# A message-passing layer on one core: copies of gathered columns from step 5 on, relu on VectorE, other places for zeros, lists and the last updates

## The chip, the core and the metric

The kernel runs on one core of one Trainium2 chip. The metric is the time of one execution in device microseconds. Engines are called PE (TensorE matmul) and PEld (its weight loads), DVE (VectorE), ACT (ScalarE), POOL (GpSimd) and SP (SyncE). POOL issues the indirect DMAs (gathers), SP most other DMAs, ACT a few.

## The reference

A graph with 12500 nodes of 64 features and 200000 edges of 32 features, the edges sorted by destination. For each edge a hidden vector of 128 is made from source node, destination node and edge; the messages are summed by destination; each node is updated, and the sum of old and new features is normalized.

```python
msg_in = concatenate([nodes[row], nodes[col], edge_features], axis=-1)   # row = src, col = dst
messages = relu(msg_in @ mW1 + mb1) @ mW2 + mb2
aggregated = segment_sum(messages, col, num_segments=12500)
upd = relu(concatenate([nodes, aggregated]) @ uW1 + ub1) @ uW2 + ub2
out = layernorm(nodes + upd)
```

## The kernel before

Edges are cut into 1563 tiles of 128, six tiles to a step (261 steps, index s), two steps to a group g of twelve tiles, for which DVE makes the selection masks. Everything is fp32.

**Tables.** Since the first layer is linear, the node parts of it are made once for every node: table A (nodes @ mW1[:64], used by source) and table B (nodes @ mW1[64:128] + mb1, used by destination), both in DRAM. `chunk_a` makes table A in thirteen chunks of eight blocks ahead of the loop (PE products, one half evacuated on ACT, L580, the other on DVE, L578, the write issued by ACT, L582). Table B is made chunk by chunk between steps (`chunk_b`, add at L588 on DVE), from step 11 to about step 50.

**A step.** `edge_part(s+1)` (L365) fills one PSUM tile `pc` with the edge and destination parts of the first layer. `node_part(s)` adds the source part: six gathers from table A (L207, one indirect DMA of 128 rows for each tile) landed in `xg`; DVE adds `xg` to `pc` and writes `h` (L392, or L388 in a copied step), and ACT applies relu to `h` (L393; L389 and L390 in a copied step). `collect(s-1)` multiplies `h` with the mask into `sums` (L420) and counts the edges (L425). In even steps `select(g+1)` makes the next masks on DVE (L233, L235, L241). The first ten steps gather node features instead and use PE for the source part (L282, L283, L381, L383).

**Copied tiles.** POOL issues one gather after another. To relieve it, some steps gather only four of their six tiles. For the other two the transposed node features are put together column by column in SBUF, in a tile `xc` of 128 columns (upper half one tile, lower half the other): `xtop` holds all nodes' features in its upper half and zeros below, `xbot` zeros above and features below, so that one column of `xc` is the sum (ACT, `singly`, L336, an activation with a bias) or the bitwise or (DVE, `joined`, L343) of one column of each. The column numbers are values in registers, loaded from the list `col_a` (L313, a register load of up to 16 values for eight copies). PE then multiplies `xc` by the weights into `pc` (L368). A step with this is a "group" in the copy plan: before, 96 of them, the first at step 16, at gaps of 3 and 2, 64 columns on ACT and 64 on DVE. The features for the second halves of `xtop` and `xbot` are loaded by `others` and their zeros written by DVE memsets in `zeros` (L562, L563), in steps 3 to 10; `columns_list` makes `col_a` in step 9.

**Order.** The order on each engine is the order of the code; waits are derived from the tiles. `xg` has nine buffers (`ROWB`): gathers of step s wait until step s-9 has been added. `pc`, `pu`, `py` and `pb` share two PSUM buffers, `h` and `xc` have two each.

**Updates.** The nodes are finished in 33 windows of up to 448 nodes (`UPD` lists the steps at which windows begin; every 4 steps near the end). `close` copies the sums (ACT, L439, L440), `update` and `activated` make the hidden layer (PE L462, L463, ACT L468), `residual` the output (PE L476, L477), `evacuate` copies it (ACT L483), `statistics`, `deviation`, `norm` (DVE L491, L493, L504, L507, ACT L498) normalize and `store` writes it, spread over the following steps.

Of the kernel before, what the change touches and what calls it, by code (L numbers as in the profile page):

```python
# [72 lines left out]
FIRST, GAPS = 16, (3, 2)  # L73
COPIED = []
while FIRST + sum(GAPS) * (len(COPIED) // len(GAPS)) + sum(GAPS[:len(COPIED) % len(GAPS)]) < NSUB - 6:
    COPIED.append(FIRST + sum(GAPS) * (len(COPIED) // len(GAPS)) + sum(GAPS[:len(COPIED) % len(GAPS)]))
RNDS = -(-len(COPIED) // len(GAPS))
LAST = 4 * (N - 1)
ACTS, CHUNK = 64, 8


def updates():


    def node(s):
        return N * min(1.0, s * SUB * P / E) ** 2
    at = [0]
    for s in range(1, NSUB):
        if s > at[-1] and node(s + 1) - node(at[-1]) > UN - WIN:
            at.append(s)  # L90
    return at
# [4 lines left out]
UL = min(UB, -(-int(N * (1 - (UPD[-1] * SUB * P / E) ** 2) + WIN) // P)) * P  # L96
# [3 lines left out]
def gnn_kernel(ctx: ExitStack, tc: tile.TileContext, x1T, x, eT, e_rows, src, src_row, dst, dst_row, wlist, wrow, wnext, whalf,  # L100
# [40 lines left out]

    cols = const.tile([RNDS * len(GAPS), 2 * P], I32, name="cols")
    col_a = const.tile([RNDS * len(GAPS), P, 2], I32, name="col_a")
# [68 lines left out]
    with tc.tile_pool(name="sup", bufs=2) as sup, tc.tile_pool(name="work", bufs=2) as work, tc.manual_schedule():  # L212
# [13 lines left out]
        def select(g, at=None):  # L226
# [11 lines left out]
            if at is not None:  # L238
                joined(at, 1, 3)
# [46 lines left out]
        def columns_list():  # L286

            for r in range(len(GAPS)):
                v = src_row[:, ((FIRST + sum(GAPS[:r])) * SUB + SUB - 2) * P:]
                nc.sync.dma_start(cols[r * RNDS:(r + 1) * RNDS],  # L290
                                  bass.AP(v.tensor, v.offset, [[sum(GAPS) * SUB * P, RNDS], [1, 2 * P]]))
            cv = cols.rearrange("k (b e) -> k b e", b=2)
            for b, base in enumerate((XBASE, YBASE)):
                nc.vector.tensor_scalar(col_a[:, :, b], cv[:, b], 4.0, float(base), op0=ALU.mult, op1=ALU.add)
# [3 lines left out]
        def portion(s, total, unit):  # L298

            rate, found = sum(GAPS) / len(GAPS), []  # L300
            begin = min(c - 2 - (j + 1) * rate for j, c in enumerate(COPIED[:len(GAPS)]))
            for j, c in enumerate(COPIED):
                lo, hi = (min(-(-int(total * (s + d - begin - j * rate) / rate * 16 + 0.5) // (16 * unit)) * unit, total) for d in (0, 1))
                lo = max(lo, 0)
                if lo < hi:
                    if c not in xc:
                        xc[c] = work.tile([P, P], F32, name="xc")
                    found.append((xc[c], j % len(GAPS) * RNDS + j // len(GAPS), lo, hi))
            return found

        def addresses(k, a, m, engine):

            _, v = nc.values_load_multi_w_load_instructions(  # L313
                col_a.rearrange("k e b -> k (e b)")[k:k + 1, 2 * a:2 * m], engines=[engine], min_val=XBASE,
                max_val=YBASE + LAST, skip_runtime_bounds_check_because="sources are node numbers")
# [15 lines left out]
        def singly(s, part, of):  # L331

            todo = [(o, k, e) for o, k, lo, hi in portion(s, ACTS, 2) for e in range(lo, hi, 2)]
# [4 lines left out]
        def joined(s, part, of):  # L338

            todo = [(o, k, ACTS + e) for o, k, lo, hi in portion(s, P - ACTS, 2) for e in range(lo, hi, 2)]  # L340
            for o, k, a, m in share(todo, part, of):
                for e, top, bot in addresses(k, a, m, ET.DVE):
                    nc.vector.tensor_tensor(o[:, e:e + 1].bitcast(I32), top.bitcast(I32), bot.bitcast(I32),  # L343
                                            op=ALU.bitwise_or)
# [26 lines left out]
        def node_part(s):  # L371
# [12 lines left out]
            else:  # L384
                a = xg.pop(s)[0].rearrange("p (b k) f -> p b k f", b=2)
                if s in COPIED:
                    m = SUB // 2 - 1
                    nc.vector.tensor_tensor(h[:, :, :m], pc[:, :, :m], a[:, :, :m], op=ALU.add)  # L388
                    nc.scalar.activation(h[:, :, :m], h[:, :, :m], AF.Relu)  # L389
                    nc.scalar.activation(h[:, :, m:], pc[:, :, m:], AF.Relu)  # L390
                for b, m in parts(n) if s not in COPIED else []:
                    nc.vector.tensor_tensor(h[:, b, :m], pc[:, b, :m], a[:, b, :m], op=ALU.add)  # L392
                    nc.scalar.activation(h[:, b, :m], h[:, b, :m], AF.Relu)  # L393
# [9 lines left out]
        def collect(s):  # L403
# [15 lines left out]
            for i in range(n):  # L419
                nc.tensor.matmul(ps[:, bass.ds(ws[i], WIN)], h[:, i % 2, i // 2, :], S[g][:, k0 + i, :],  # L420
                                 start=False, stop=ends and i == n - 1)
            if s == 0 or period[s - 1] != u:
                nc.tensor.matmul(pn, zero_b[:, 0:1], zero_b, start=True, stop=False)
            for i in range(n):
                nc.tensor.matmul(pn[:, bass.ds(ws[i], WIN)], one, SB[g][:, k0 + i, :, 1], start=False,  # L425
                                 stop=ends and i == n - 1)

# [8 lines left out]
        def close(u):  # L436

            ps, pn = sums.pop(u)
            nc.scalar.copy(sums_s[u % 2], ps)  # L439
            nc.scalar.copy(xw[u % 2][0:1, :UW], pn)  # L440
# [7 lines left out]
        def blocks(u):  # L448
            return UB if u + 1 < K else UL // P
# [8 lines left out]
        def update(u):  # L458
# [3 lines left out]
            nc.tensor.matmul(pu, w2u, sums_s[u % 2][:, :n], start=True, stop=False)  # L462
            nc.tensor.matmul(pu, uz, xw[u % 2][:, :n], start=False, stop=True)  # L463
# [8 lines left out]
        def residual(u):  # L472

            py = psum.tile([P, UB, D], F32, name="py", tag="pc")
            for i in range(blocks(u)):
                nc.tensor.matmul(py[:, i], xw[u % 2][:, i * P:(i + 1) * P], ux, start=True, stop=False)  # L476
                nc.tensor.matmul(py[:, i], hT[:, i * P:(i + 1) * P], u2, start=False, stop=True)  # L477
# [166 lines left out]
        for k, c in enumerate(range(0, NB, NCH)):  # L644
            chunk_a(c)
            if k == 0:
# [103 lines left out]
        for s in range(last + 2):  # L750
# [6 lines left out]
            def earlier(n):  # L757

                return next((u for d, u in due.items() if u + 1 < K and s - d == n - (u + 2 == K and n > 2)), None)
            if tail:  # L760
                norm(K - 1)
            if s + 2 < NSUB:
                windows(s + 2)
            if s < NSUB:
                node_part(s)
                joined(s, 0, 3 if j == 0 and g + 1 < NSUP else 2)
# [3 lines left out]
            if 1 <= s <= NSUB:  # L770
                collect(s - 1)
            if s + 1 in due:
# [11 lines left out]
            if s in due:  # L784
# [15 lines left out]
            joined(s, 2 if j == 0 and g + 1 < NSUP else 1, 3 if j == 0 and g + 1 < NSUP else 2)  # L800
            singly(s, 0, 1)
            if s in due and due[s] + 1 < K:
# [175 lines left out]
```

## Time and profile before

| | us |
|---|---|
| median of three runs | 1740.07 (1739.24 to 1740.65) |
| the profiled execution, its own time | 1740.13 |
| its span, from the first to the last instruction | 1738.4 |
| busy: PE, PEld | 1451.4, 1261.2 |
| busy: DVE, ACT | 1076.5, 1442.8 |
| busy: POOL | 1299.3 |
| mean granted TensorE clock | 0.574 of full speed |

Busy time is the time in which an engine executes; the reading and loading of registers, branches and the issue of DMAs do not count. A line of a group says line, engine, operation, tiles (out<-in), shapes and count, then busy us and mean ns of one, and behind the second bar the idle time of the engine just before such instructions, with what ended it. "issue" there is idle time in which the engine waited for nothing that the profile shows. In a timeline a line says start, duration, engine, line, operation, and in brackets the idle time ahead.

### The profile page before, as it was taken

Reading aid. Unit: us, or ns where it says so; the run is one execution under the profiler, and the core shown is the slowest. Engines: PE = TensorE matmul, PEld = TensorE weight load, DVE = VectorE, ACT = ScalarE, POOL = GpSimd, SP = SyncE. Lnnn points to the kernel's source line nnn. Section 1 sums busy time; section 2 is a strip of 40 time slices with the busy share of each in tenths; the row PEclk is TensorE's granted clock in tenths of the full one; section 3 lists DMA queues with packets and bytes.
Section 4 is the critical chain, followed back from the end, with each engine's and each line's share of the span. In section 5 each row is a group of like instructions: output and inputs, shape, how many; then the busy total and the mean of one; then the engine's idle time right before and its main releaser. Section 6 shows DMA issues by size and latency. Waiting matters only on the chain. (4 is left out here: it accounts for less than half of the span.)

```text
span 1738.4 us, 46326 instructions
## 1 busy us (share of the span) xinstructions
PE 1451.4 (83%) x9598; PEld 1261.2 (73%) x9598; DVE 1076.5 (62%) x7325; ACT 1442.8 (83%) x6691; POOL 1299.3 (75%) x1380
## 2 busy tenths in 40 slices
PE   3697888888888887887988889898888888889997
PEld 2586777878777776766877777687777667777775
DVE  1566766767676656666666666666666666666642
ACT  0216998999999888988999999999999999899941
POOL 7777777777777777777777777777777777777774
PEclk8665555565555555555555555555556656565665
DMA  8773434433333333333333333333333334343342
GB/s 214 207 160 103 124 105 128 120 92 100 101 97 98 95 97 94 98 101 95 99 107 103 104 107 104 105 106 104 105 108 109 106 109 111 104 111 110 108 111 63
DMA packets 207110, 192.27 MB, mean 111 GB/s; under 512 B 57098, under 2 KB 172931, under 8 KB 206835
## 3 DMA queue, kind: packets, MB, share of 16 engines
q1 hardware_dynamic: 148418, 92.38, 19.5%
q0 software_dynamic: 43872, 87.97, 18.5%
q10 hardware_dynamic: 14546, 8.93, 1.8%
q8 instruction: 91, 1.49, 0.4%
q14 instruction: 183, 1.50, 0.3%
HBM read 171.46 MB, written 17.66 MB: 109 GB/s over the span
## 5 line engine op out<-in xcount | busy, mean ns | idle before, releaser
L207 POOL DMA_INDIRECT xg<-tab_a,src_s x1311 | 1240.8, 946 | 399.6 <-issue 361.4
L336 ACT ACTIVATE xc<-xtop,xbot 128x1 f32 x6144 | 1167.3, 280 | 41.0 <-issue 29.8
L343 DVE TENSOR_TENSOR xc<-xtop,xbot 128x1 int32 x6144 | 536.7, 154 | 410.0 <-issue 397.1
L420 PEld LDWEIGHTS sums<-sel,h 128*128 128x128 f32 x3126 | 620.3, 299 | 73.8 <-ACT h L393 27.6
L420 PE MATMUL sums<-sel,h 128*128 128x32 f32 x3126 | 643.7, 373 | 27.0 <-ACT h L393 20.2
L365 PE MATMUL pc<-rhs,l 64*128 64x128 f32 x3126 | 424.7, 418 | 183.3 <-DVE h L392 128.3
L365 PEld LDWEIGHTS pc<-rhs,l 64*128 64x128 f32 x3126 | 353.1, 297 | 248.2 <-DVE h L392 144.9
L393 ACT ACTIVATE h<-h 128x768 f32<-128x768 f32 x156 | 129.6, 831 | 128.5 <-DVE h L392 127.9
L392 DVE TENSOR_TENSOR h<-pc,xg 128x768 f32<-128x768 f32 x156 | 148.0, 949 | 128.7 <-DMA xg<-tab_a,src_s 77.9
L235 DVE TENSOR_TENSOR l<-l,cps 128x768 f32<-128x768 int32 (+1 forms) x134 | 127.8, 953 | 7.8 <-DMA l<-in_dst_row 2.5
L425 PE MATMUL cnt<-sel,one 128*1 128x32 bf16 x1563 | 84.5, 187 | 0.0
L388 DVE TENSOR_TENSOR h<-pc,xg 128x512 f32<-128x512 f32 x96 | 66.1, 689 | 22.2 <-DMA xg<-tab_a,src_s 8.7
L241 DVE TENSOR_TENSOR sel<-cps,drc 128x384 f32<-128x384 f32 x131 | 71.6, 547 | 12.0 <-PE cnt L425 11.8
L368 PE MATMUL pc<-w1a,xc 64*128 64x128 f32 x384 | 74.3, 395 | 0.0
L462 PE MATMUL pu<-sums_s,w2u 128*128 128x448 f32 (+1 forms) x66 | 61.2, 1031 | 15.5 <-DVE h L392 14.9
L207 POOL DMA_INDIRECT xg<-in_x,src_s x60 | 57.5, 958 | 19.1 <-issue 18.0
L425 PEld LDWEIGHTS <-one 128*1 128x1 bf16 x1563 | 53.9, 83 | 22.1 <-issue 8.7
L476 PE MATMUL py<-ux,xw 128*128 128x64 f32 x262 | 66.3, 344 | 1.8 <-DVE h L392 1.8
L389 ACT ACTIVATE h<-h 128x512 f32<-128x512 f32 x96 | 59.2, 617 | 9.3 <-DVE h L388 9.0
L368 PEld LDWEIGHTS pc<-w1a,xc 64*128 64x128 f32 x384 | 66.2, 308 | 0.0
L477 PE MATMUL py<-u,hTu 128*128 128x64 f32 x262 | 65.0, 340 | 0.3 <-ACT hTu L468 0.3
L476 PEld LDWEIGHTS py<-ux,xw 128*128 128x128 f32 x262 | 53.0, 250 | 7.7 <-issue 3.1
(104 smaller groups left out, 749.4 us busy)
## 6 DMA issues: line engine op xcount, KB each, us to landing
l<-in_dst_row SPq DMA_DIRECT2D x262, 96.0 KB
l<-in_eT SPq DMA_DIRECT2D x262, 96.0 KB
xg<-tab_a,src_s POOLq DMA_INDIRECT x1311
rhs<-tab_b SPq DMA_DIRECT2D x361, 32.0 KB
tab_b<-tb SPq DMA_DIRECT2D x13, 512.0 KB
rhs<-tab_b SPq DMA_DIRECT2D x387, 16.0 KB
tab_a<-tb ACTq DMA_DIRECT2D x12, 512.0 KB
out<-y SPq DMA_DIRECT2D x32, 128.0 KB
```

Of the source, the lines that this page charges most:

```text
L207: nc.gpsimd.indirect_dma_start(out=a[:, i, :] if s < XG else a[:, i // 2, i % 2, :], out_offset=None, in_=A[:, :] if s >= XG else x[:, :], ...
L235: nc.vector.tensor_tensor(l[r], l[r].bitcast(I32), node[r].unsqueeze(2).broadcast_to([r.stop - r.start, SUP // 2, P]), op=ALU.is_equal)
L241: nc.vector.tensor_tensor(s[:, :nt], slot.unsqueeze(1).broadcast_to([P, nt, WIN]), drc[:, g * SUP:g * SUP + nt].unsqueeze(2).broadcast_to( ...
L336: nc.scalar.activation(o[:, e:e + 1], top.bitcast(F32), AF.Identity, bias=bot.bitcast(F32))
L343: nc.vector.tensor_tensor(o[:, e:e + 1].bitcast(I32), top.bitcast(I32), bot.bitcast(I32), op=ALU.bitwise_or)
L365: nc.tensor.matmul(pc[:, b, k, :], L[g][q:q + 64, m, :], rhs[g % 2][q:q + 64, w, :], start=s >= XG or k == 0, stop=s >= XG and not copied)
L368: nc.tensor.matmul(pc[:, b, k, :], xc[s][q:q + 64], w1a[q:q + 64], start=False, stop=True)
L392: nc.vector.tensor_tensor(h[:, b, :m], pc[:, b, :m], a[:, b, :m], op=ALU.add)
L393: nc.scalar.activation(h[:, b, :m], h[:, b, :m], AF.Relu)
L420: nc.tensor.matmul(ps[:, bass.ds(ws[i], WIN)], h[:, i % 2, i // 2, :], S[g][:, k0 + i, :], start=False, stop=ends and i == n - 1)
L425: nc.tensor.matmul(pn[:, bass.ds(ws[i], WIN)], one, SB[g][:, k0 + i, :, 1], start=False, stop=ends and i == n - 1)
L476: nc.tensor.matmul(py[:, i], xw[u % 2][:, i * P:(i + 1) * P], ux, start=True, stop=False)
```

## The change

- The copy plan: 110 groups instead of 96. Copying begins in step 5 (`BEGIN`), at a rate of 0.47 groups a step that falls to 0.42 (`RATES`). The first group is step 10, the last 254, and a group's copies end three steps ahead of it. ACT makes 68 of the 128 columns, DVE 60. Even steps get more of DVE's copies than odd ones (`SWING`).
- In `node_part` DVE adds `xg` into `pc` itself (PSUM) and then makes the relu from `pc` into `h`. Register loads for copies are placed between add and relu and behind the relu (`fetch`), the copies of both after that (`join`); eight more copies stand in `select`, and what is left of the step's share at the step's end.
- `zeros` are written by ACT, 14 pairs of 896 columns, one after each chunk of table A and two after the last. `others` go to steps 0 to 2, `columns_list` to step 2, and the list covers all steps.
- `collect` counts first and sums afterwards; `close` copies the counts first; `update` starts with the product of `xw`; `residual` makes all products of `xw` first.
- The last updates: windows begin at steps 244, 248, 252, 256 and 259 where they began at 245, 249, 253 and 257 (34 windows, the last one 192 nodes wide instead of 384). The update of the last window but one is made in one piece in step 259, ahead of that step's add.

```diff
-FIRST, GAPS = 16, (3, 2)
+BEGIN, FINAL = 5, 255
+RATES = 0.47, 0.42
+SWING = 0.04
+def progress(s, early=0.0):
+    s = max(s + 1 - BEGIN, 0)
+    return s * (RATES[0] + (RATES[1] - RATES[0]) * s / (2 * NSUB)) + (early if s else 0.0)
 COPIED = []
+for s in range(NSUB):
+    while min(progress(s), progress(s, -SWING if s % 2 else SWING)) >= len(COPIED) + 1 and s + 3 < FINAL:
+        COPIED.append(s + 3)
-ACTS, CHUNK = 64, 8
+ACTS, CHUNK = 68, 8
...
 def select(g, at=None):
-                joined(at, 1, 3)
+                join(fetch(quota(at), CHUNK))
...
+        def fetch(todo, n):
+            ready = []
+            while todo and n:
+                o, c, a = todo[0]
+                m = min(len([t for t in todo if t[1] == c]), n // 2)
+                del todo[:m]
+                n -= 2 * m
+                ready += [(o, *x) for x in addresses(c, a, a + 2 * m, ET.DVE)]
+            return ready
+        def join(ready):
+            for o, e, top, bot in ready:
+                nc.vector.tensor_tensor(o[:, e:e + 1].bitcast(I32), top.bitcast(I32), bot.bitcast(I32),
+                                        op=ALU.bitwise_or)
...
 def node_part(s):
-                if s in COPIED:
-                    m = SUB // 2 - 1
-                    nc.vector.tensor_tensor(h[:, :, :m], pc[:, :, :m], a[:, :, :m], op=ALU.add)
-                    nc.scalar.activation(h[:, :, :m], h[:, :, :m], AF.Relu)
-                    nc.scalar.activation(h[:, :, m:], pc[:, :, m:], AF.Relu)
-                for b, m in parts(n) if s not in COPIED else []:
-                    nc.vector.tensor_tensor(h[:, b, :m], pc[:, b, :m], a[:, b, :m], op=ALU.add)
-                    nc.scalar.activation(h[:, b, :m], h[:, b, :m], AF.Relu)
+                m = SUB // 2 - (s in COPIED)
+                todo = quota(s)
+                if n == SUB:
+                    nc.vector.tensor_tensor(pc[:, :, :m], pc[:, :, :m], a[:, :, :m], op=ALU.add)
+                    ready = fetch(todo, CHUNK - 2 * (s in COPIED))
+                    nc.vector.tensor_scalar(h, pc, 0.0, None, op0=ALU.max)
...
+                join(ready + fetch(todo, CHUNK))
...
 def zeros(i, n):
-            nc.vector.memset(xtop[D:, i * w:(i + 1) * w], 0.0)
-            nc.vector.memset(xbot[:D, i * w:(i + 1) * w], 0.0)
+            for t in (xtop[D:], xbot[:D]):
+                nc.scalar.activation(t[:, i * w:(i + 1) * w], ident[:D, 0:1].broadcast_to([D, w]), AF.Copy, scale=0.0)
...
             chunk_a(c)
+            for i in range(k, 14 if c + NCH >= NB else k + 1):
+                zeros(i, 14)
...
 def rest(s):
-            if 3 <= s < 9 and s % 2:
-                others((s - 3) // 2 * 4, (s - 3) // 2 * 4 + 4)
-            if 3 <= s < 11:
-                zeros(s - 3, 8)
-            if s == 9:
+            if s < 3:
+                others(s * 4, s * 4 + 4)
+            if s == 2:
                 columns_list()
...
+            if s == UPD[K - 1]:
+                for stage in (evacuate, statistics, deviation, norm, store):
+                    stage(K - 3)
+                collect(s - 1)
+                for stage in (close, update, activated, residual, evacuate):
+                    stage(K - 2)
             if s < NSUB:
                 node_part(s)
-                joined(s, 0, 3 if j == 0 and g + 1 < NSUP else 2)
...
             rest(s)
-            joined(s, 2 if j == 0 and g + 1 < NSUP else 1, 3 if j == 0 and g + 1 < NSUP else 2)
+            while s < NSUB and quota(s):
+                join(fetch(quota(s), CHUNK))
             singly(s, 0, 1)
```

In lines of the changed kernel L417 is the add and L419 the relu of `node_part`, L369 DVE's copies, L346 those of ACT, L323 the register loads, L596 the zeros and L218 the gathers.

More of the change, by code (lines that the diff above doesn't have):

```diff
@@ L336, in singly, with quota @@
                     nc.scalar.activation(o[:, e:e + 1], top.bitcast(F32), AF.Identity, bias=bot.bitcast(F32))
[L338 to L344, printed above, removed]
+        def quota(s):
+            if s not in quotas:
+                early = [-SWING if (s + d) % 2 else SWING for d in (-1, 0)]
+                quotas[s] = [(o, c, ACTS + e) for o, c, lo, hi in portion(s, P - ACTS, early) for e in range(lo, hi, 2)]
+            return quotas[s]
+        def fetch(todo, n):
[11 more added lines that the diff above has]
+                                        op=ALU.bitwise_or)
+        quotas = {}
         xc = {}
@@ L426, in collect @@
                                  stop=ends and i == n - 1)
+            for i in range(n):
+                nc.tensor.matmul(ps[:, bass.ds(ws[i], WIN)], h[:, i % 2, i // 2, :], S[g][:, k0 + i, :],
+                                 start=False, stop=ends and i == n - 1)
         def carry(u):
```

77 lines of the change are left out of this document (40 added, 37 removed).

## The prediction

> **What bounds the kernel now.** I read the page's table of groups first, then the engines' idle time, then the timeline of POOL, DVE and ACT in the middle of the run, and last the end of the chain of waits. From the page (busy us and mean ns of one, then idle before it):
>
> ```profile
> L207 POOL DMA_INDIRECT xg<-tab_a,src_s x1311 | 1240.8, 946 | 399.6 <-issue 361.4
> L336 ACT ACTIVATE xc<-xtop,xbot 128x1 f32 x6144 | 1167.3, 280 | 41.0 <-issue 29.8
> L343 DVE TENSOR_TENSOR xc<-xtop,xbot 128x1 int32 x6144 | 536.7, 154 | 410.0 <-issue 397.1
> L393 ACT ACTIVATE h<-h 128x768 f32<-128x768 f32 x156 | 129.6, 831 | 128.5 <-DVE h L392 127.9
> ```
>
> POOL looks 75% busy, but it is full. Each gather takes 0.944 us and is followed by 0.30 us of "issue", so one starts every 1.2475 us. 1371 gathers at that pitch are 1710 us, and the trace has the first at 2.8 and the last at 1717.7, with only 5.8 us lost on the way. The timeline of POOL shows the pitch and the largest single loss:
>
> ```profile
> 119.37 0.94 POOL L207 DMA_INDIRECT xg<-tab_a,src_s  x1 [0.30 <-issue]
> 120.61 2.46 POOL L207 DMA_INDIRECT xg<-tab_a,src_s  x1 [0.30 <-issue]
> 123.38 0.95 POOL L207 DMA_INDIRECT xg<-tab_a,src_s  x1 [0.30 <-issue]
> ```
>
> From about step 80 on each step's add starts 2.6 to 4 us after its last gather was issued: the consumers follow POOL. Before that they do not. Step 0's relu is at 73.9 us, when POOL is nine steps ahead, and the others catch up at 6.15 us a step (step 20 at 192.2, step 50 at 376.7) while POOL needs 6.49. In that stretch the timeline of DVE (start, duration, idle before) is the one to read, here steps 58, 59 and the start of 60:
>
> ```profile
> 423.28 0.96 DVE L392 TENSOR_TENSOR h<-pc,xg 128x768 f32<-128x768 f32 x1
> 424.50 0.67 DVE L343 TENSOR_TENSOR xc<-xtop,xbot 128x1 int32 x8 [0.27 <-issue]
> 425.10 0.21 DVE L233 TENSOR_SCALAR cps<-wh,pidx 128x6 f32<-128x6 int32 x1
> 425.35 0.95 DVE L235 TENSOR_TENSOR l<-l,cps 128x768 f32<-128x768 int32 x1
> 426.57 0.69 DVE L343 TENSOR_TENSOR xc<-xtop,xbot 128x1 int32 x8 [0.26 <-issue]
> 427.18 0.54 DVE L241 TENSOR_TENSOR sel<-cps,drc 128x384 f32<-128x384 f32 x1
> 428.07 0.65 DVE L343 TENSOR_TENSOR xc<-xtop,xbot 128x1 int32 x8 [0.35 <-issue]
> 428.64 0.68 DVE L388 TENSOR_TENSOR h<-pc,xg 128x512 f32<-128x512 f32 x1
> 429.87 0.64 DVE L343 TENSOR_TENSOR xc<-xtop,xbot 128x1 int32 x8 [0.55 <-issue]
> 431.11 0.51 DVE L343 TENSOR_TENSOR xc<-xtop,xbot 128x1 int32 x6 [0.60 <-issue]
> 432.53 0.65 DVE L343 TENSOR_TENSOR xc<-xtop,xbot 128x1 int32 x8 [0.91 <-issue]
> 433.50 0.37 DVE L343 TENSOR_TENSOR xc<-xtop,xbot 128x1 int32 x4 [0.33 <-issue]
> 434.01 0.96 DVE L392 TENSOR_TENSOR h<-pc,xg 128x768 f32<-128x768 f32 x1
> ```
>
> DVE waits for nobody here, yet it idles between chunks of copies. The idle time is the register load (L313) of the next chunk's addresses: 1.10 us for 16 values (0.85 for 12, 0.60 for 8, 0.35 for 4), begun some 0.3 us after the chunk before it starts, and 0.09 us from its end to the first copy. So eight copies cost 1.4 to 1.5 us where the load is bare, and 0.6 us where it runs under an operation of 0.95 us, as after L235. DVE therefore needs 5.4 us for these steps and 5.8 on average from step 60 to 78, against POOL's 6.49. That is the slack that the change spends.
>
> **The change, part by part.** The profiled execution took 1740.1 us (span 1738.4), the same as the median.
>
> *Gathers.* 110 groups instead of 96, two gathers each: 28 fewer, 28 x 1.2475 = 34.9 us off POOL's queue. POOL's need falls to about 6.32 us a step early (rate 0.47) and 6.42 late (0.42).
>
> *Relu from ACT to DVE.* ACT loses 129.6 + 59.2 + 34.7 = 223.5 us (L393, L389, L390) and its tie to every step. It gains 1336 copies (7480 instead of 6144) at the 0.185 us between starts in the timeline: 247 us. Per step that is at most 0.47 x 68 x 0.185 = 5.9 us, plus 2.3 us for each update (0.2 to 0.5 a step): under POOL's need, so I cost it at nothing except at the head. DVE gains one 128x768 operation from PSUM in some 250 steps: L578's 0.69 us for 512 columns and L392's 0.95 for 768 give 0.95. Its add now writes PSUM. No row shows that; I take the same 0.95 (a slip of 0.1 either way would move a step by nothing to 0.1, since the load behind it is longer). The relu is less than it looks, because loads are placed under it: add, load, relu at +1.22, load, copies at +2.45 in one run of 16. Hand sum from the rows above for an even step with 32 copies: 2.45 + 1.17 for the 16, then L233 and L235 with a load under the latter (1.48), eight copies 0.6, L241 with its bare load 1.5 minus what overlaps, eight copies: 7.2 us. An odd, copied step with 22: add 0.68 and a load of 12, relu at +0.97, copies at +2.2, 14 of them 1.0, bare load, eight copies: 4.85. Together 12.0 us for 54 copies, 6.0 a step, where before had 10.7 for 50. So DVE has 0.65 us more to do in a step.
>
> *Updates.* 2.16 us on DVE each (L491, L493, L504, L507 over 32 updates), 30 of them in the last 210 steps: 0.31 a step, about half of it over loads in flight. DVE's pace from step 50 is then 6.15 to 6.3, against POOL's 6.38.
>
> *Head.* The zero halves move from 16 DVE memsets of 1.36 us to 28 ACT operations of 896 columns, by L393's slope about 0.94 us each, 1.9 a chunk. Behind them on ACT stand the next chunk's copy and the issue of its table write. Chunks then need 1.75 + 1.9 = 3.65 us on ACT. Where the timeline has them 2.2 to 3.9 apart (from 56 us on) they slip, and the last chunk has two pairs behind it: first transposed copy at 81 instead of 71.6, +9.4. The last table write slips by 5.6 us; it had landed at 75.0 and the first gather from the table was at 78.6, so POOL loses 2. Against this the 1.5 us that POOL lost at 120.61, where a memset of 1.36 us started at 120.81, go. Lists and column loads moved to steps 0 to 2 stand on SP ahead of the window loads, 2.6 us for the lists: covered, since DVE has only selections there; 3 us if not. Copies in steps 5 to 9 make ACT's step 5.9 + 0.81 + 0.48 = 7.2 us where it was 6.65: +3 to 4.
>
> *What is late next: row buffers.* A gather of step s needs step s-9 done. At step 25 POOL now has 14.4 us of room. The change brings its gather 7.5 us forward (three more copied steps by then), and the consumers come later by 9.4 + 4 + 15 steps x 0.65, less 2.7 for the memsets: 20. So 14.4 - 7.5 - 20: POOL waits 13 us. Up to step 50 the consumers, with table B's chunks (1.2 us of DVE each), run at 6.5 to 6.8 against 6.33: 4 to 12 more. I take 18 in all (5 to 30). At step 50 the consumers are nine steps behind and must make up some 50 us in 210 steps. At a pace of 6.15 to 6.17 they leave about 6 us (0 to 45).
>
> *End.* From the last gather to the end are 20.7 us. The last update shrinks from 384 to 192 columns, its first product leaves the path (1.29), the second halves (-0.8), a block of three goes (-1.1 over hT, py and statistics), and the eight products of the update before it no longer stand ahead of the last sums (-1.4): -4.6. One more update costs PE 9.6 us, beside its slack: PE's twelve sums take 2.77 us at 1618.4 and 1.48 at 1613.3, so it has speed in hand.
>
> Sum: 1740.1 - 34.9 - 4.6 + 2 - 1.5 + 18 + 6 = 1725; with POOL's first 2 us inside the 18, 1723.
>
> **Rivals.** *No early wait* (DVE quicker than the hand sum, buffers last): 1740.1 - 34.9 - 1.5 - 4.6 = 1699. For it: before, no gather waited for a buffer. Against it: the room above.
>
> *DVE becomes the bound; slower.* If its pace stays at 6.3 or more from step 50 on, it never catches up. Step 50 at 376.7 + 9.4 + 4 + 40 x 0.8 = 422, then 210 x 6.3 = 1323, then 14 from the last add to the end and 1.7 around the span: 1761; at 6.4, 1782. It decides from a pace of 6.25 (412 + 210 x 6.25 + 15.7 = 1740). For it: every stall that DVE shows before (1.0 us before L392 at 1609, waits for copy buffers) now falls into no slack. Against it: steps 50 to 78 show DVE within 0.2 us of such sums.
>
> *The relu locks POOL out.* The 2.46 us gather beside a memset shows that DVE can hold POOL up for its own length. If each of 250 relus did so for even 0.4 us, +100: 1820. The Trainium skill (SBUF — State Buffer, "Who interferes with whom") says that a tensor_scalar in a two-port mode shuts GpSimd out, and names tensor_scalar, which the relu is; by that rule 1820. The same skill (VectorE: DVE Perf Modes, "Why PSUM operands drop a tier") rules that mode out for a PSUM operand; the trace agrees so far as L578, a copy of 512 columns from PSUM, takes 0.69 us, just as long as the adds of 512 columns (L388).
>
> **How the numbers follow.** Early wait, then POOL to the end (1723): 0.45. No early wait (1699): 0.13. DVE the bound (1745 to 1785): 0.37. Lock: 0.02. Gains and losses cancel (within 0.2%, 3.5 us, about what a measurement can tell): the rest, and parts of the first and third, 0.08 together. Faster by more: 0.54, slower by more: 0.38. The range leaves out the lowest and highest tenth: 1697 to 1772. The first case alone spans 1704 to 1737.
>
> **What would show it.** Gathers 1343 at 1.2475 us; a few of them between 130 and 400 us waiting for DVE's add (L417) by some 18 us in all; pairs of steps of 12.0 to 12.3 us on DVE after 400 us; the first L294 copy near 81; 16 us from the last gather to the end. Gaps in POOL all through, with DVE's add late, would prove the third case. A pace above 6.25 makes this forecast wrong.

## The result, and the profile after

The change makes the kernel slower: 1937.75 us (median of four runs, 1933.74 to 1940.26) against 1739.67 (1739.24 to 1740.65), a ratio of 1.1139 with an interval of 1.1125 to 1.1153. The profiled execution took 1933.7 us, its span 1932.0, at a mean granted TensorE clock of 0.551 (0.574 before). The time lies far above the forecast (1723 us, range 1697 to 1772).

The groups of the page that answer to those shown of before, and one of the update's products (busy us and mean ns of one, then idle before them and what ended most of it):

```profile
L218 POOL DMA_INDIRECT xg<-tab_a,src_s x1283 | 1211.2, 944 | 568.2 <-issue 347.3
L346 ACT ACTIVATE xc<-xtop,xbot 128x1 f32 x7480 | 1404.7, 280 | 106.9 <-issue 68.8
L369 DVE TENSOR_TENSOR xc<-xtop,xbot 128x1 int32 x6600 | 535.7, 153 | 324.6 <-issue 234.5
...
L419 DVE TENSOR_SCALAR h<-pc 128x768 f32<-128x768 f32 x250 | 239.3, 957 | 75.8 <-DVE pc L417 67.9
...
L508 PE MATMUL py<-ux,xw 128*128 128x64 f32 x268 | 63.6, 417 | 138.4 <-DVE h L419 138.4
```

The operations that the forecast priced cost about what it said. The relu takes 0.957 us (0.95 forecast), and the gather 0.944 us (0.946 before). What is new stands behind the second bars. POOL's idle time grew from 399.6 to 568.2 us. PE stood 138.4 us ahead of `py`, the output product of an update, and DVE's relu ended every one of those waits. Before, the same product waited 1.8 us:

```profile
L476 PE MATMUL py<-ux,xw 128*128 128x64 f32 x262 | 66.3, 344 | 1.8 <-DVE h L392 1.8
```

The waits of after say it once more (waiting engine and line, releaser, us in all, times, longest):

```profile
POOL xg L218 <- DVE pc L417: 192.4, 89, 7.8
...
PE py L508 <- DVE h L419: 138.4, 30, 7.2
```

The timeline around the update of step 115 shows how one leads to the other (start, duration, engine and line, and in brackets the idle time ahead):

```profile
861.76 1.65 PE L393 MATMUL pc<-rhs,l 64*128 64x128 f32 x12 [1.20 <-issue]
...
867.45 0.96 DVE L417 TENSOR_TENSOR pc<-pc,xg 128x768 f32<-128x768 f32 x1
...
868.69 0.96 DVE L419 TENSOR_SCALAR h<-pc 128x768 f32<-128x768 f32 x1 [0.28 <-DVE pc L417]
...
869.79 1.94 PE L508 MATMUL py<-ux,xw 128*128 128x64 f32 x8 [6.38 <-DVE h L419]
...
871.52 1.91 PE L510 MATMUL py<-u,hTu 128*128 128x64 f32 x8
...
873.62 2.77 PE L457 MATMUL sums<-sel,h 128*128 128x32 f32 x12
...
876.32 1.65 PE L393 MATMUL pc<-rhs,l 64*128 64x128 f32 x12
...
878.07 0.97 DVE L417 TENSOR_TENSOR pc<-pc,xg 128x768 f32<-128x768 f32 x1 [6.11 <-DMA xg<-tab_a,src_s]
...
879.31 0.94 POOL L218 DMA_INDIRECT xg<-tab_a,src_s  x1 [2.67 <-DVE pc L417]
```

PE makes the edge sums of step 117 at 861.76, and the next thing on its queue is `py`. `py` needs nothing of step 117, yet it starts 0.14 us after that step's relu has ended. Behind it stand the sums of step 116 and the edge sums of step 118. DVE's add of step 118 comes when these are through, after 6.11 us in which DVE had nothing to do. (The profile names the gather's DMA as releaser, but these gathers were issued nine steps earlier; the edge sums end at 877.97, 0.1 us before the add, and fit better.) POOL, nine row buffers ahead, then waits for that add. Measured between the starts of the adds over the 30 updates that have at least four steps to the next, the step behind `py` takes 11.20 us in the trace of after, and 6.44 in that of before: 143 us over 30 updates.

The reason is in the program as it was built. `pc`, `pu`, `py` and `pb` share two buffers in PSUM, the memory into which PE writes its products, and which of the two a tile gets is settled when the program is made. In the kernel before, `py` never got the buffer of the `pc` taken just before it (0 of 33 updates). In the kernel after it did so in 30 of 34. No line of the change gives it one of the two: the only line on buffers puts the `py` of the last window but one elsewhere, with the `sums`. A `py` on the buffer of step 117's `pc` has to wait until that is read for the last time, and that now happens in the relu. The lower granted clock does not explain these waits: run g2 below, with the same operations and a clock of 0.550, takes 1801 us once the buffers are named.

DVE's own work, steps 58 and the start of 59, answers to the stretch shown of before:

```profile
479.88 0.97 DVE L417 TENSOR_TENSOR pc<-pc,xg 128x768 f32<-128x768 f32 x1
481.13 0.96 DVE L419 TENSOR_SCALAR h<-pc 128x768 f32<-128x768 f32 x1 [0.29 <-DVE pc L417]
482.39 1.25 DVE L369 TENSOR_TENSOR xc<-xtop,xbot 128x1 int32 x16 [0.30 <-issue]
483.56 0.21 DVE L244 TENSOR_SCALAR cps<-wh,pidx 128x6 f32<-128x6 int32 x1
483.81 0.95 DVE L246 TENSOR_TENSOR l<-l,cps 128x768 f32<-128x768 int32 x1
485.07 0.72 DVE L369 TENSOR_TENSOR xc<-xtop,xbot 128x1 int32 x8 [0.30 <-issue]
485.71 0.54 DVE L252 TENSOR_TENSOR sel<-cps,drc 128x384 f32<-128x384 f32 x1
486.70 0.65 DVE L369 TENSOR_TENSOR xc<-xtop,xbot 128x1 int32 x8 [0.44 <-issue]
487.26 0.69 DVE L417 TENSOR_TENSOR pc<-pc,xg 128x512 f32<-128x512 f32 x1
```

The loads run under the relu as the hand sum had it: this even step takes 7.38 us (7.2 in the sum), the odd one behind it 4.48 (4.85), together 11.87 against 12.0. And the 2.46 us gather is gone from POOL's timeline at the same place:

```profile
119.08 0.94 POOL L218 DMA_INDIRECT xg<-tab_a,src_s  x1 [0.30 <-issue]
120.33 0.94 POOL L218 DMA_INDIRECT xg<-tab_a,src_s  x1 [0.30 <-issue]
```

The prediction took that gather for one held up by a memset. The other memsets do not bear this out: of before's sixteen, fourteen lie beside gathers of 0.94 to 0.95 us only and one also beside a gather of 1.35, and in h1 below, where all sixteen are back, no gather beside them takes over 1.12 us. The gather of 2.46 us also lies beside two short DVE operations on the list `col_a` (L294 of before, 122.10 to 122.39 us), but in h1 these lie beside gathers of at most 0.95 us. The change moved both; what held that gather stays open.

### The profile page after: what moved, and what is told of

The parts are those of the page before. It is cut to its first block, busy times and chain, and to the rows that moved or that the text cites. A ratio compares the mean times of both kernels' runs of the same rounds, so it can differ in the third digit from the quotient of the medians.

```text
span 1932.0 us, 48263 instructions
## 1 busy us (share of the span) xinstructions
PE 1545.9 (80%) x9676; PEld 1339.5 (69%) x9676; DVE 1288.6 (67%) x8037; ACT 1516.8 (79%) x7712; POOL 1269.8 (66%) x1352
## 4 chain that ended last, share of the span: by engine, by line
DVE 31%; PE 23%; POOL 15%; issue 14%; DMA 9%; DVEq 5%; ACT 2%; ACTq 0%; SPq 0%; POOLq 0%
POOL xg L218 15%; DVE xc L369 12%; PE sums L457 8%; DVE h L419 7%; DVE pc L417 6%; PE pc L393 5%; DVEq L323 5%; DMA xg<-tab_a,src_s 5%; DVE l L246 3%; PE py L508 3%; PE py L510 2%; DMA tab_a<-tb 1%; PE pu L494 1%; DVE sel L252 1%; PE pu L495 1%
## 5 line engine op out<-in xcount | busy, mean ns | idle before, releaser
L218 POOL DMA_INDIRECT xg<-tab_a,src_s x1283 | 1211.2, 944 | 568.2 <-issue 347.3
L346 ACT ACTIVATE xc<-xtop,xbot 128x1 f32 x7480 | 1404.7, 280 | 106.9 <-issue 68.8
L369 DVE TENSOR_TENSOR xc<-xtop,xbot 128x1 int32 x6600 | 535.7, 153 | 324.6 <-issue 234.5
L457 PE MATMUL sums<-sel,h 128*128 128x32 f32 x3126 | 671.5, 383 | 10.8 <-DVE h L419 9.9
L457 PEld LDWEIGHTS sums<-sel,h 128*128 128x128 f32 x3126 | 637.2, 308 | 29.6 <-DVE h L419 13.3
L393 PE MATMUL pc<-rhs,l 64*128 64x128 f32 x3126 | 445.2, 428 | 163.3 <-DMA l<-in_eT 49.1
L393 PEld LDWEIGHTS pc<-rhs,l 64*128 64x128 f32 x3126 | 371.9, 305 | 228.2 <-issue 172.6
L419 DVE TENSOR_SCALAR h<-pc 128x768 f32<-128x768 f32 x250 | 239.3, 957 | 75.8 <-DVE pc L417 67.9
L417 DVE TENSOR_TENSOR pc<-pc,xg 128x768 f32<-128x768 f32 (+1 forms) x250 | 211.3, 845 | 103.2 <-PE pc L393 57.5
L508 PE MATMUL py<-ux,xw 128*128 128x64 f32 x268 | 63.6, 417 | 138.4 <-DVE h L419 138.4
L218 POOL DMA_INDIRECT xg<-in_x,src_s x60 | 57.6, 960 | 19.1 <-issue 17.7
L494 PE MATMUL pu<-xw,uz 128*128 128x448 f32 (+1 forms) x68 | 61.5, 1008 | 2.1 <-DVE h L419 1.1
L510 PEld LDWEIGHTS py<-u,hTu 128*128 128x128 f32 x268 | 59.5, 325 | 0.0
```

Of the source, the lines that this page charges most:

```text
L218: nc.gpsimd.indirect_dma_start(out=a[:, i, :] if s < XG else a[:, i // 2, i % 2, :], out_offset=None, in_=A[:, :] if s >= XG else x[:, :], ...
L346: nc.scalar.activation(o[:, e:e + 1], top.bitcast(F32), AF.Identity, bias=bot.bitcast(F32))
L393: nc.tensor.matmul(pc[:, b, k, :], L[g][q:q + 64, m, :], rhs[g % 2][q:q + 64, w, :], start=s >= XG or k == 0, stop=s >= XG and not copied)
L417: nc.vector.tensor_tensor(pc[:, :, :m], pc[:, :, :m], a[:, :, :m], op=ALU.add)
L419: nc.vector.tensor_scalar(h, pc, 0.0, None, op0=ALU.max)
```

## The experiments

Theory A: `py` shares a buffer with the edge sums of the next step, and this takes most of the loss. Theory B: DVE has too much to do with relu and copies, wherever the buffers lie. Each run is told with its ratio to the kernel before on the same chip. An update is due one step after the next window begins; its `py` comes one step later, behind the edge sums of the step after that. "Step behind py" is the mean time from the add two steps after the due step to the next add, over updates at least four steps ahead of the next. "Other steps" leaves out the five steps around each update, from one ahead of the due step to three behind it. Both count from step 50 on.

| run | us | before, same chip | ratio (95%) | py on the last pc's buffer | step behind py | other steps |
|---|---|---|---|---|---|---|
| before | 1739.67 | | 1 | 0 of 33 | 6.44 | 6.17 |
| after | 1937.75 | 1739.67 | 1.1139 (1.1125 to 1.1153) | 30 of 34 | 11.20 | 6.14 |
| e1_act_first | 1795.11 | 1743.13 | 1.0300 (1.0283 to 1.0317) | 0 of 34 | 6.74 | 6.13 |
| e2_before_relu | 1935.81 | 1743.13 | 1.1099 (1.1080 to 1.1117) | 28 of 33 | 9.91 | 6.62 |
| e3_before_collide | 1787.09 | 1743.13 | 1.0255 (1.0238 to 1.0273) | 33 of 33 | 9.84 | 5.94 |
| e4_before_relu_act_first | 1829.81 | 1743.13 | 1.0496 (1.0479 to 1.0514) | 0 of 33 | 6.49 | 6.62 |
| g1_acts76_zeros | 1860.40 | 1739.56 | 1.0699 (1.0681 to 1.0717) | 2 of 34 | 7.08 | 5.64 |
| g2_buffers_named | 1801.15 | 1739.65 | 1.0349 (1.0323 to 1.0374) | 0 of 34 | 6.81 | 6.13 |
| g3_rebalanced | 1745.71 | 1739.65 | 1.0036 (1.0022 to 1.0051) | 0 of 34 | 6.80 | 5.81 |
| h1_old_head | 1724.09 | 1740.34 | 0.9905 (0.9890 to 0.9921) | 0 of 34 | 6.61 | 5.70 |
| h2_old_head_end | 1721.81 | 1740.34 | 0.9900 (0.9885 to 0.9914) | 0 of 33 | 6.70 | 5.77 |
| h3_110_groups | 1767.39 | 1739.38 | 1.0158 (1.0143 to 1.0174) | 0 of 33 | 7.05 | 5.97 |

### The shared buffer

**e1_act_first.** The kernel after, with one call moved:

```diff
-            singly(s, 0, 1)
             if s in due and due[s] + 2 < K:
                 activated(due[s])
+            singly(s, 0, 1)
```

> The kernel after, with one call moved: ACT's relu of an update (activated) is issued ahead of the copies of its step instead of behind them. In the program so built, py no longer gets the PSUM buffer of the pc that was taken just before it in any update (0 of 34; 30 of 34 in the kernel after). Theory A (py shares a buffer with the edge sums of the next step, so PE stands until that step's relu is through, and the sums and edge sums behind it come late): the step behind py falls from 11.2 us to about 6.4 in 30 updates, 145 us, so 1775 to 1800 us, and PE py L508 waits for DVE h by under 10 us in all (138 in the kernel after). Theory B (DVE simply has too much to do with relu and copies): 1925 to 1945, the same stalls in other places.

Measured 1795, as theory A had it. The step behind `py` is back at 6.74 us, and `py` no longer waits. But moving the call brings waits of its own, since ACT now stands for PE ahead of its copies:

```profile
ACT hTu L500 <- PE pu L495: 108.3, 32, 8.7
```

**g2_buffers_named** does without these waits. No call is moved; the two buffers get names, and a rule in the program alternates them but for the second `pc` behind a `pu`, so that `py` takes what `pu` left:

```diff
+    turns, near = [0], []
+    def bank(kind="pc"):
+        if kind[:2] in ("pw", "pf"):
+            return f"pc{1 - turns[-1]}"
+        keep = kind == "pc" and near[-2:] == ["pu", "pc"]
+        near.append(kind)
+        turns.append(turns[-1] if keep else 1 - turns[-1])
+        return f"pc{turns[-1]}"
...
-            py = psum.tile([P, UB, D], F32, name="py", tag="sums" if u + 2 == K else "pc")
+            py = psum.tile([P, UB, D], F32, name="py", **({"tag": "sums"} if u + 2 == K else {"tag": bank("py"), "bufs": 1}))
```

> The kernel after with no call moved: only the two PSUM buffers of pc, pu, py and pb are named in the program, so that py takes the one that pu left and not that of the pc taken before it (0 of 34). ACT's activation stays behind the copies. The first run moved that call and showed 1795, but in it ACT stood 108 us waiting for PE's pu ahead of its copies. Theory A (the shared buffer is the loss): the step behind py falls from 11.2 to 6.4 to 6.8 us, and the time is that of the first run or lower, 1770 to 1800. Theory B: 1925 to 1945.

1801, just above the case of theory A, with every operation and every order of the kernel after. It is no faster than e1 (ratios 1.0349 and 1.0300), so ACT's waits in e1 cost nothing that shows. 137 of the 198 us lost are the shared buffer. The Trainium skill (Perfetto Trace Analysis, "Matmuls") says that independent groups of products should rotate through different PSUM banks, so that one is read while the next is made. This pair of runs agrees, and gives a case in which a kernel written to rotate did not.

**e2_before_relu and e4_before_relu_act_first** come from the other side: the kernel before with only add and relu as in the kernel after, and the same with the activation moved.

```diff
-                if s in COPIED:
-                    m = SUB // 2 - 1
-                    nc.vector.tensor_tensor(h[:, :, :m], pc[:, :, :m], a[:, :, :m], op=ALU.add)
-                    nc.scalar.activation(h[:, :, :m], h[:, :, :m], AF.Relu)
-                    nc.scalar.activation(h[:, :, m:], pc[:, :, m:], AF.Relu)
...
+                m = SUB // 2 - (s in COPIED)
+                if n == SUB:
+                    nc.vector.tensor_tensor(pc[:, :, :m], pc[:, :, :m], a[:, :, :m], op=ALU.add)
+                    nc.vector.tensor_scalar(h, pc, 0.0, None, op0=ALU.max)
...
```

> The kernel before with one change: add into pc in place and relu on DVE, as in the kernel after; copies, lists, zero halves and updates stay. In its program py shares the buffer of the pc taken before it in 28 of 33 updates. Theory A: 28 x 4.8 = 134 us lost in the steps of updates, of which POOL's slack of 0.3 us a step gives some 30 to 60 back: 1810 to 1870 us. Theory B: DVE has four copies a step fewer than in the kernel after, its pace by the hand sum is about 6.0 to 6.2 against POOL's 6.49: 1738 to 1760.

> As the run before this but one (the kernel before with relu on DVE), with the update's ACT relu issued ahead of the copies; py then shares no buffer with the pc before it in any of 33 updates. Theory A: the loss of that run is gone: 1738 to 1760 us. Theory B: the same time as that run.

The relu with its add in place makes the kernel before as slow as the whole change does, 1936 us, and brings `py` onto the wrong buffer without any other part of the change. That the two times are alike is chance, for they add up differently. With the buffers mended it is 1830: 106 us were the buffers. But neither theory had the other 87. In e4 the other steps take 6.62 us, above POOL's 6.49. Between 420 and 1640 us DVE waits there for other engines and DMAs under 7 us in all, and stands 276 us ahead of its copies for register loads: this part is DVE's work. In the change's order, with loads under the relu, the other steps take 6.13 us with more groups (e1).

**e3_before_collide** asks what sharing costs without the relu. It is the kernel before with buffers named so that `py` always takes that of the `pc` before it:

```diff
+        keep = kind == "py" or kind == "pc" and (near[-3:-1] == ["pu", "pc"] or near[-3:-1] == ["py", "pc"])
```

> The kernel before, relu on ACT as it was, with the PSUM buffers of pc, pu and py named so that they follow the order of the kernel after (py on the buffer of the pc taken before it in 33 of 33 updates; 0 of 33 in the kernel before). Nothing else is changed. Theory A, buffers alone: PE waits in py for the next step's add, which frees pc, then come the sums and the next edge sums, as in the kernel after; the add frees pc some 3 us sooner than the relu does there, so 2 to 3 us per update and 1745 to 1800 us. If sharing costs only together with the late release by the relu: 1738 to 1745. Theory B: no change, 1738 to 1742.

1787, 44 us slower, so sharing costs by itself. `py` waits for the add where that frees `pc`, and in copied steps for ACT's relu of the last third:

```profile
PE py L487 <- DVE h L403: 74.5, 21, 4.9
...
PE py L487 <- ACT h L401: 52.0, 10, 5.9
```

The step behind `py` grows by 3.4 us, as much as in e2. Yet POOL waits for no buffer on the way, and the loss shows only behind its last gather: 63.5 us instead of 20.7. The consumers had 0.3 us a step to spare and used it up.

### What is left: DVE's pace, the split and the head

In g2 POOL loses 50 us in waits, 42 of them before 500 us, and the end comes 68 us after its last gather. The consumers are nine steps behind to the end. None of them has much left: of the 510 us between 1130 and 1640 in e1, DVE stands some 51, ACT 41 and PE 35, with the idle time that ends in "issue" ahead of copies, the register loads, counted as work. Whose pace that is was to be told by runs with relu on ACT, zero halves on DVE, 76 columns on ACT, and 96 groups, all on top of e1 or after:

> The kernel after with the relu of pc into h back on ACT, everything else as it is (add into pc in place, 110 groups, zero halves on ACT). In its program py shares no buffer with the pc before it (0 of 34). DVE loses 0.957 us a step. If DVE's work is what is left of the loss once the buffers are right (first run: 1795), DVE falls to 5.2 us a step and ACT, with 0.42 to 0.47 x 68 copies x 0.185 us, 0.83 for the relu and 2.3 per update, needs 6.4 to 7.1: 1740 to 1790, bound by ACT and POOL. If not DVE but PE or the head holds the first run: 1790 to 1800.

> The first run's kernel (activation ahead of the copies), with the zero halves written by DVE memsets at the same place instead of by ACT. The first transposed copy, at 85.8 us in the first run and at 71.6 before the change, should come near 73 to 76. If the consumers (DVE and PE) hold the kernel from the head to the end, the 10 to 13 us go through to the end: 1782 to 1787. If POOL holds it at the end, as the forecast had it: 1793 to 1797, no change.

> As the run before this one (zero halves on DVE, activation ahead of the copies), and ACT makes 76 of a group's 128 columns, DVE 52 instead of 60: 3.4 to 3.8 copies a step fewer on DVE, at about 0.14 us with their share of the loads some 0.5 us a step. py shares its buffer in 2 of 34 updates. If DVE's work sets the pace: 6.46 falls to 6.0 to 6.2 and POOL's 6.32 to 6.44 takes over, 1715 to 1745. If PE, or waits between PE and DVE, set it: within 10 us of the run before.

> The first run's kernel with rates of 0.41 falling to 0.366, which gives 96 copied groups as before the change instead of 110: POOL has 28 gathers more (35 us), DVE some 840 copies fewer (3.2 a step, 0.45 us). If DVE sets the pace: the pace falls below POOL's 6.5, and the time is POOL's, 1735 to 1760. If PE sets it: PE loses 0.34 us for each copied group less, 5 us in all, so 1785 to 1795.

They were run on a chip on which the kernel before took 2517 us, and again as f1_relu_act to f4_rate96 on another, where it took 2496. PE, DVE and ACT of these runs stand for issue (PE's weight loads 505 us in e6, where e1 has 178). Ratios were 1.0436, 1.0320, 1.0395 and 1.0436, then 1.0326, 1.0337, 1.0380 and 1.0388. The kernel of e7 and f3 is also that of g1 below, whose ratio, where the kernel before takes 1740 us, is 1.0699. So these ratios do not carry over, and they are not used.

> The kernel after with the relu of pc into h back on ACT, everything else as it is (add into pc in place, 110 groups, zero halves on ACT); again, since the chip of the run before ran every kernel 45% longer. py shares no buffer with the pc before it (0 of 34). DVE loses 0.957 us a step. If DVE's work is what is left of the loss once the buffers are right (first run: 1795), DVE falls to 5.2 us a step and ACT, with 0.42 to 0.47 x 68 copies x 0.185 us, 0.83 for the relu and 2.3 per update, needs 6.4 to 7.1: 1740 to 1790, bound by ACT and POOL. If not DVE but PE or the head holds the first run: 1790 to 1800.

(f2 to f4 expected what e6 to e8 did.) So relu on ACT, the zero halves by themselves and the lower rate by itself stay untested.

**g1_acts76_zeros**, the kernel of e7 on a faster chip: as e1, with `ACTS` 76 instead of 68 and the zero halves by DVE memsets.

> The kernel after with the update's activation ahead of the copies, zero halves by DVE memsets at the same place, and 76 of a group's 128 columns by ACT, 52 by DVE (60 before): 3.4 to 3.8 copies a step fewer on DVE, some 0.5 us a step with their share of the loads. py shares its buffer in 2 of 34 updates. The first run (1795) had its last gather at 1723.8 and its end 69 us later: the consumers were nine steps behind POOL all the way. If DVE's work sets their pace: they get below POOL's 6.42 us a step, and the tail behind the last gather shrinks to 16 to 30 us, 1715 to 1745. If PE (93% busy between 1380 and 1640 us in the first run), or ACT, sets it: 1775 to 1795.

Slower, 1860, outside both expectations, and still it answers: the steps away from updates fall from 6.13 to 5.64 us with eight columns fewer on DVE, the 0.5 us expected. DVE's work sets the pace there. What is new is a stall at each update on PE, here in its timeline:

```profile
1280.19 0.58 PE L432 MATMUL sums<-zero_b 128*128 128x480 bf16 x1
1285.59 0.56 PE L452 MATMUL cnt<-zero_b 128*1 128x480 bf16 x1 [4.81 <-ACT xw L471]
```

The counts have one PSUM buffer, which ACT empties when its queue of copies lets it: 102.7 us in 28 waits. ACT was full: it stood 14 of the same 510 us, again with the loads counted as work.

**g3_rebalanced**: g2 with 72 columns on ACT, rates 0.44 to 0.40 (103 groups), zero halves by DVE memsets.

```diff
-RATES = 0.47, 0.42
+RATES = 0.44, 0.4
-ACTS, CHUNK = 68, 8
+ACTS, CHUNK = 72, 8
-                nc.scalar.activation(t[:, i * w:(i + 1) * w], ident[:D, 0:1].broadcast_to([D, w]), AF.Copy, scale=0.0)
+                nc.vector.memset(t[:, i * w:(i + 1) * w], 0.0)
```

> The run before this one with less copying and another split: rates 0.44 to 0.40 (103 groups, 14 gathers more for POOL, 17.5 us), 72 of 128 columns by ACT and 56 by DVE, and the zero halves by DVE memsets at the same place. DVE loses 1.7 copies a step by the split and 1.1 by the rate, some 0.4 us a step, and ACT's copies come to 0.43 x 72 x 0.185 = 5.7 us a step. If DVE's pace left the consumers nine steps behind: 6.46 falls to 6.05 to 6.15, below POOL's 6.47, the lag is made up and the tail behind the last gather is 16 to 30 us: 1725 to 1745. If ACT holds it as in the run with 76 columns, or PE: 1760 to 1800.

1746, 1 us above the first case. DVE now waits for the gathers, as it should where POOL is the bound, and 23.9 us lie behind the last gather. From its waits:

```profile
DVE pc L428 <- DMA xg<-tab_a,src_s: 76.0, 39, 6.1
```

Three things changed at once, so no run tells how much of the 55 us from g2 each gave; the other steps fall from 6.13 to 5.81 us. With 14 gathers fewer than before it is still 6 us slower: POOL lost 22 us before 190 us. The largest gap is the first gather from table A, at 87.5 us where it was at 78.6:

```profile
87.54 0.94 POOL L218 DMA_INDIRECT xg<-tab_a,src_s  x1 [8.90 <-DMA tab_a<-tb]
```

So the zero halves cost there whichever engine writes them; they stand among the evacuations of table A.

**h1_old_head and h2_old_head_end**: g3 with the old head (zeros in steps 3 to 10, copies from step 12, 104 groups), then with the old last updates as well.

```diff
-BEGIN, FINAL = 5, 255
-RATES = 0.44, 0.4
+BEGIN, FINAL = 12, 255
+RATES = 0.46, 0.41
...
-            for i in range(k, 14 if c + NCH >= NB else k + 1):
-                zeros(i, 14)
...
-            if s < 3:
-                others(s * 4, s * 4 + 4)
-            if s == 2:
+            if 3 <= s < 9 and s % 2:
+                others((s - 3) // 2 * 4, (s - 3) // 2 * 4 + 4)
+            if 3 <= s < 11:
+                zeros(s - 3, 8)
+            if s == 9:
                 columns_list()
```

> The run before this one (buffers named, 72 columns by ACT, 56 by DVE) with the head of the kernel before: zero halves by DVE memsets in steps 3 to 10, the other columns in steps 3, 5 and 7, the list in step 9, and copies from step 12 on (first copied group 17); rates 0.46 to 0.41 give 104 groups, one more. That run lost 22 us of POOL's queue, all of it before 190 us: 8.6 at the first gather from table A and 13 where buffers were not free. If the head made those, POOL loses 2 to 4 us in all, the last gather is at 1355 x 1.2475 + 2.8 + 3 = 1696 to 1700, and with the 24 us behind it 1720 to 1727. If the waits for buffers come from DVE's relu, not from the head, they stay: 1735 to 1745.

> As the run before this one with the last updates as in the kernel before (33 instead of 34, the last of 384 columns instead of 192, their stages in the old order). The forecast had the new end 4.6 us shorter. The trace of the rebalanced run has 23.9 us from its last gather to the end, 20.7 in the kernel before: statistics and norm of the update before stand ahead of the last adds on DVE, and the last update's columns land 1.1 us late. If the forecast's sum holds: 4 to 5 us longer than the run before this one. By the trace: 1 to 4 us shorter.

1724 and 1722: both beat the kernel before by 1%. Against its pitch of 1.2475 us a gather POOL loses 3.8 and 5.1 us on the way, where it lost 5.8 before. It waits for no buffer any more (longest idle stretch 0.3 us, here in h1):

```profile
POOL xg L218 <- issue: 376.8, 1236, 0.3
```

The head was 22 us, 2.5 of which are h1's one more group. The end is 22.3 us from the last gather with the old updates and 26.4 with the new ones, in the profiled executions; the 2.3 us between the times of the two kernels lie within their intervals.

**h3_110_groups**: h2 with rates 0.48 to 0.44, as many groups as the kernel after has.

> As the last run (old head, old end, buffers named, 72 columns by ACT) with rates 0.48 to 0.44, which give 110 groups, as many as the kernel after, instead of 104: 12 gathers, 15 us, fewer on POOL. Between steps 120 and 200 the last two runs' adds came every 6.26 to 6.30 us while they still made up their lag. POOL would need 6.36 to 6.41. If the consumers keep 6.3 with 0.8 copies a step more on DVE (0.1 us) and 1.1 on ACT (0.2 us), POOL stays the bound: 1704 to 1712. If they fall behind, the tail behind the last gather grows from 22 us towards 60: 1715 to 1740.

1767, above both cases: 46 us slower than h2, not faster by the 15 us of its 12 gathers. POOL waits for the adds again, and 56.6 us lie behind its last gather:

```profile
POOL xg L216 <- DVE pc L426: 30.0, 30, 4.7
```

The other steps take 5.97 us instead of 5.77. Between 104 and 110 groups the consumers fall behind POOL.

## Why the prediction was wrong

**The step that failed first: PE costed at nothing.** "PE's twelve sums take 2.77 us at 1618.4 and 1.48 at 1613.3, so it has speed in hand", and the relu on DVE was priced by its length alone. Its second effect was left out: the add no longer frees `pc`, the relu does, 1.24 us later in the stretch shown, and the buffers that four kinds of tiles share are dealt anew. The runs put 137 us on this (after against g2). No rival had it. Even without it the forecast fails: g2's 1801 us lies above the range too. It could have been seen without any run, in the program as built, by asking for each tile which tile had its buffer before, and by whose last reading it comes free.

**The second: the lag is made up.** The forecast let the consumers run at 6.15 to 6.17 from step 50 on, with each update at 2.16 us of DVE, half of it over loads. With the buffers mended (g2) the steps away from updates are 6.13, near the 6.0 summed, but the five steps around an update take 32.8 us, 2.2 more than five others: as much as all of the 2.16, not half. The mean pace is 6.46 from step 50 to 258. The second rival's own sum, step 50 at 422 and 210 steps and 15.7 us, gives 1794 at this pace; g2 has step 50 at 420.7 and ends at 1801. So the third case, chance 0.37, was how it went once the buffer is taken out, at a pace that the forecast had named as the point where it decides (6.25), and with a price bounded too low (1785).

**The third: the head.** The zero operations take 0.95 us, as estimated (0.94), but the last write of table A is issued at 81.1 us instead of 71.2, 9.9 later and not 5.6. The first gather from the table stands for it until 84.1, and POOL loses 5.5 us there, not 2. The first transposed copy is at 85.2 us instead of 81, and step 10's add comes 20.4 us later than before, where 9.4 and 4 were added up. The waits of POOL between 100 and 400 us come to 30 us in after (18 forecast, 5 to 30 as bounds) and 28 in g2.

**The end: -4.6 was wrong in sign or nothing.** In h1 statistics and norm of the update before stand ahead of the last adds on DVE, and the load of the last update's columns, 1.77 us, lies on the chain ahead of its first product. The rearranged end is 4 us longer than the old one in the two traces.

**What held.** 1343 gathers at 1.2475 us; the relu at 0.957 (0.95); the add into PSUM at 0.97, as long as into SBUF; a pair of DVE steps 11.87 us (12.0); the gather of 2.46 us gone. The term of 34.9 us for 28 gathers holds at its size only as long as POOL is the bound: h2's 16 fewer gathers are 20.0 us by it, and the kernel is 18.5 faster. At 110 groups it was not to be had with either split tried (68 or 72 columns on ACT). The lock did not come: the gather's mean is 0.944 us beside 250 relus. This agrees with what the Trainium skill (VectorE: DVE Perf Modes, "Why PSUM operands drop a tier") says of operands in PSUM.

**What stays open.** By what rule the program's making deals the two buffers: the runs show that the engine of the relu and the place of one ACT call in the order change it, not why. Nor was relu on ACT with the rest of the change tried on a chip where it can be read. The new order of counts, sums and update products stands in every run built on after, so what it is worth by itself is not shown.

## What to carry to other kernels

An operation that moves to another engine also moves the moment at which its operand's buffer comes free; look for each shared buffer who gets it next, before and after the change, and name the buffers in the program if the rotation matters. Cost every engine's whole queue around the periodic work (here the updates), not only the plain steps: with three engines standing some 50 of 510 us or less there is no place left for it. A term that shortens the bounding queue is worth its size only up to the point where the consumers' pace meets it; h2 and h3 lie six groups apart and 46 us.

## What was not expected of the hardware

On two chips the kernel before took 43 to 45% longer (2517 and 2496 us), and the kernel of g1 39 to 41% (2614 and 2590 against 1860). PE, DVE and ACT stand for issue there, while the gather takes 0.944 to 0.947 us as everywhere. The four kernels tried on them came out at 1.03 to 1.04 times the kernel before, g1's among them, which is at 1.07 elsewhere. Why these chips are slower stays open.
